# A graph layer on one core: left-over nodes moved to the front, the x part of layer 1 moved ahead of the last slots, iteration 0 written out

## The chip, the cores and the metric

One core of one Trainium2 chip runs the whole kernel. The metric is the device time of one execution in microseconds (us). Before the change it is 276.57 us, the median of three runs (276.30 to 278.17).

## The reference, cut to what matters

```python
agg = jax.ops.segment_sum(edges, recv, num_segments=N_NODES)   # edges [412500, 48] -> [12500, 48]
u = graph_globals[batch]                                       # batch is all zero: one row for every node
h0 = jnp.maximum(_layernorm(x, axis=-1), 0.0)                  # x [12500, 128]
h = jax.nn.relu(jnp.concatenate([h0, agg, u], axis=1) @ W1 + b1)   # 240 -> 256
return x + h @ W2 + b2                                         # 256 -> 128
```

Everything is float32. `recv` (`dst` in the kernel) is sorted, and each node has 33 edges on average (412,500 / 12,500).

## The kernel before, in words

**Chunks, groups, slots.** The edges are cut into chunks of 768 (128 partitions of 6 edges), four chunks make a group, and 1,024 nodes with 11 groups make an iteration. Twelve iterations cover 12,288 nodes and groups 1 to 132; group 0 comes ahead of them and groups 133 and 134 (six chunks) behind them, with the last 212 nodes, called Z or "the rest". In an iteration the 11 groups sit in six slots (`SLOTS`), two groups in each but slot 4. Each slot has its own buffers for edges (`e`), one-hots (`oh`), windows (`pl`) and partial sums (`ss`), and an edge buffer is loaded again, for the next iteration, as soon as the sums that read it are done.

**The segment sum as matmuls.** `onehot` (L662) builds on VectorE, for each edge, a row of 28 that marks its node relative to the chunk's first node. `add_up` (L681) multiplies edges by one-hots on TensorE (L685) and ScalarE copies the sums out of PSUM (L689). `windows` (L669) builds on VectorE where a chunk's 28 sums lie in a window of 186 nodes, and `place` (L695) multiplies the sums by these windows into the aggregate banks `ax` and `ay` (L707), 512 nodes each. A window that crosses the edge of a bank is two matmuls (`pieces`, L44).

**The dst values.** `dst_1`, `dst_2` and `dst_3` (L578 to L611) turn `dst` into the relative positions `rel` and the offsets `off`: for each of five blocks of 128 chunks VectorE casts and subtracts (L583, L586), TensorE transposes (L600), ScalarE copies (L601), and TensorE and VectorE make the offsets (L593, L609). `fetch` and `fetch_off` copy one iteration's part of them.

**The node part.** For each half of an iteration, A and B (512 nodes each): `stats`, `variance` and `shift` on VectorE with a root on ScalarE, `norm` on ScalarE (L735), `turn` transposes on TensorE (L744) with a copy on ScalarE (L745), `layer_x` (L754) and `layer_e` (L759) make layer 1 in banks `ph` and `pt`/`po`, `relu` (L764) on ScalarE, `second` (L780) makes layer 2 into `ph`, VectorE adds x and b2 into `hold` (L784), and all held results are stored at the end. `add_b` (L739) on GpSimd adds b2 to x. `sums_out` (L750) on ScalarE copies the aggregates for `layer_e`.

**What sets the order.** `Flow` collects all operations in one list. Each engine runs its own in the list's order, and `order` works out the semaphore waits from what each operation reads and writes. `run` emits all that stands ahead of iteration 0, then a hardware loop over the iterations for every engine. TensorE has a loop of its own, whose round is cut at `f.mark`: it begins with slot 4 of the iteration before and ends with slot 3. An iteration on TensorE is: sums of slots 0, 1, 2; placing of slot 5's bank 0, slot 0's bank 1 and slot 1; layer 2 of the iteration before, A and B; sums of slot 3, (round ends) 4, 5; the transposes; placing of slots 2, 3, 4, 5; x part; edge part. In iteration 0 layer 2 works on zeros that ScalarE wrote first. The load of the next x is issued by ScalarE after the copies of the transposes; the edge loads by SyncE. In the prologue SyncE issues the five dst blocks, group 0, slots 0 and 1, x, the other slots. The epilogue sums, places and transforms the rest, between the last edge part and the last layer 2, and stores.

Of the kernel before, what the change touches and what calls it, by code (L numbers as in the profile page):

```python
# [13 lines left out]
OP = mybir.AluOpType  # L14
# [18 lines left out]
BACK = 46  # L33
# [21 lines left out]
class Flow:  # L55
# [22 lines left out]
    def order(self, loop):  # L78
# [15 lines left out]
        for o in self.seq:  # L94
# [19 lines left out]
            for n in sorted(deps, reverse=True):  # L114
# [5 lines left out]
                if not inside(o):  # L120
# [31 lines left out]
        self.at_lo = {o["name"]: o["count"] for o in self.seq if o["it"] == lo}  # L152
# [38 lines left out]
    def run(self):  # L191
# [5 lines left out]
        body = [o for o in self.seq if o["it"] == lo]  # L197
        end = [o for o in self.seq if o["it"] is not None and o["it"] > hi]
        for e in self.of:
            self.prepare(e)  # L200
        self.straight([o for o in start if o["eng"] != "PE"])
        regs = {}
        for o in body:
            for n, back in self.body.get(o["name"], []):
                u = self.unit(n)
                key = (o["eng"], u, (self.at_lo[n] - lo - back + self.extra[n]) * u)
                if key not in regs:
                    r = self.of[o["eng"]].alloc_register(f"w_{o['eng']}_{len(regs)}")
                    self.of[o["eng"]].reg_mov(r, key[2] + lo * u)
                    regs[key] = r  # L210

        def ahead(e):
            for n, c in sorted(self.ahead[e].items()):
                self.of[e].wait_ge(self.sem[n], (self.rank[n, c] + self.extra[n]) * self.unit(n))
# [13 lines left out]
        others = [e for e in self.of if e != "PE"]  # L228
        for e in others:
            ahead(e)  # L230
        every = {o["name"] for o in self.seq if o["it"] == hi}
        with nc.Fori(lo, hi + 1, 1, engines=[self.of[e].engine for e in others]) as i:
            for e in others:
                mine = [o for o in body if o["eng"] == e]
                for always, some in groupby(mine, lambda o: o["name"] in every):
# [7 lines left out]
        own = [o for o in body if o["eng"] == "PE"]  # L243
        cut = [o["name"] for o in own].index(self.mark)
        with nc.Fori(0, hi - lo + 2, 1, engines=[nc.tensor.engine]) as j:
# [7 lines left out]
            with nc.tensor.If(j < hi - lo + 1):  # L253
                for o in own[:cut]:
                    repeat(o, None)
# [152 lines left out]
def kernel(  # L408
# [25 lines left out]
    RC = NCH - (NIT * GI + 1) * CG  # L434
    RN = N - NIT * IN
    assert TAIL == TP * T and 0 < RN <= BN and RN % RZ == 0 and RN // RZ <= P
    assert CG < RC <= 2 * CG and IN * (E // N) == IE
# [20 lines left out]
    rel = const.tile([P, ((NIT + 1) * GI + 1) * q], F32)  # L458
    off = const.tile([P, (NIT + 1) * GI + 1], F32)
# [8 lines left out]
    two = (("a", R), ("b", R), ("r", RZ))  # L468
    RR = [r for _, r in two]
    xt = [const.tile([P, r, D], F32, name=f"x{k}") for k, r in two]  # L470
# [5 lines left out]
    ot = [const.tile([P, r, D], F32, name=f"ot{k}") for k, r in two]  # L476
# [5 lines left out]
    hold = [const.tile([P, max(NIT - 1, n) * R * D], F32, name=f"hold{k}") for k, n in (("a", -(-(NB + DF) * CE // (R * D))), ("b", 0))]  # L482
    ssr = const.tile([P, 2, DE], F32)
# [13 lines left out]
    zero = const.tile([P, 1], F32)  # L497
    base = const.tile([P, NIT + 1, GI], F32)
# [8 lines left out]
    fc = [const.tile([P, 1], F32, name=f"fc{k}") for k in range(NB)]  # L507
    mf = [const.tile([P, P // CG], F32, name=f"mf{k}") for k in range(NB)]
# [14 lines left out]
    def load_dst(b):  # L523
# [5 lines left out]
        if full < rows:  # L529
            n = CE // TAIL  # L530
            dma("SP", f"ld{b}r", [], [k + "r"], d[full:rows, :n * TAIL].rearrange("a (n e) -> a n e", e=TAIL),
                dst[None, None, E - TAIL:E].to_broadcast([1, n, TAIL]))
            dma("SP", f"ld{b}s", [], [k + "s"], d[full:rows, n * TAIL:], dst[None, E - TAIL:E - TAIL + CE - n * TAIL])
# [4 lines left out]
    def load_e(s, j, only=None):  # L538

        for k, g in enumerate(SLOTS[s]):  # L540
            if only not in (None, k):
                continue
            dma("SP", f"le{s}.{k}", [], [f"e{s}.{k}"], e[s][:, k * CG:(k + 1) * CG],
# [475 lines left out]
```

## Time and profile before

| what | number |
|---|---|
| median of the runs | 276.57 us |
| the profiled execution: its own time | 279.47 us |
| its span, first to last instruction | 277.7 us |
| TensorE busy, VectorE busy | 256.6 us (92%), 239.2 us (86%) |
| ScalarE busy, GpSimd busy | 127.6 us (46%), 54.5 us (20%) |
| read from HBM, mean rate over the span | 87.75 MB, 339 GB/s |

A row of a group or of the order in time names start, length, engine, source line, operation, output and input tiles with their shapes, and a count; in brackets stand the engine's idle time ahead of it and what ended that. PEld is the weight load of a matmul. A float32 matmul appears as two. "issue" marks time in which the engine waited for nothing that the profile shows.

### The profile page before, as it was taken

The numbers are of one execution on the slowest core, as the hardware profiler recorded it, in microseconds if no ns is written. First come the engines' busy times: TensorE is split into PE (matmuls) and PEld (weight loads), VectorE is DVE, ScalarE is ACT, GpSimd is POOL, SyncE is SP. The second block draws the span as 40 slices with busy tenths as digits, with TensorE's granted clock in tenths as the row PEclk, the third lists the DMA queues.
The fourth block names the chain that finished last, engine by engine and source line by source line (L and its number), as shares of the span: only waits on it lengthen the run. The fifth ranks groups of instructions, "written<-read, shape, count | busy, mean of one in ns | idle before, by whom it ended". The sixth has DMA issues, their size and how long they took to land.

```text
span 277.7 us, 17205 instructions
## 1 busy us (share of the span) xinstructions
PE 256.6 (92%) x7567; PEld 198.7 (72%) x7568; DVE 239.2 (86%) x591; ACT 127.6 (46%) x316; POOL 54.5 (20%) x47
## 2 busy tenths in 40 slices
PE   2787999999999999999999999999999999999991
PEld 2676867858849859768678588497596686785690
DVE  4599999999989989989989899899899799898211
ACT  7710535537347345445363383473454443633510
POOL 8100050140500500501303105005005023043000
PEclk9855899999999999999999999999999999999868
DMA  6999999999999999999999999999999999979402
GB/s 205 319 389 385 371 388 391 390 393 374 389 393 320 390 372 332 390 311 390 392 302 390 393 311 388 392 310 390 361 323 390 327 385 392 308 284 382 173 23 75
DMA packets 79012, 94.33 MB, mean 340 GB/s; under 512 B 3227, under 2 KB 72189, under 8 KB 78998
## 3 DMA queue, kind: packets, MB, share of 16 engines
q1 hardware_dynamic: 75398, 87.63, 90.0%
q10 hardware_dynamic: 3312, 6.03, 5.7%
q0 software_dynamic: 288, 0.49, 0.7%
q8 instruction: 7, 0.11, 0.2%
q14 instruction: 7, 0.06, 0.1%
HBM read 87.75 MB, written 6.40 MB: 339 GB/s over the span
## 4 chain that ended last, share of the span: by engine, by line
PE 88%; DMA 4%; SPq 3%; issue 3%; DVE 0%
PE s L685 28%; PE ph L780 18%; PE ph L754 8%; PE ax L707 7%; PE ph L759 5%; PE po L754 4%; PE pt L754 4%; DMA e<-in_edge_attr_dram 4%; PE pt L759 4%; PE ay L707 3%; SPq L520 3%; PE pt L744 3%; PE po L744 2%; PE s L942 1%; PE s L754 1%
## 5 line engine op out<-in xcount | busy, mean ns | idle before, releaser
L666 DVE TENSOR_TENSOR oh<-iota_v,rel_i 128x1344 f32<-128x1344 f32 (+1 forms) x78 | 130.7, 1715 | 0.0
L685 PEld LDWEIGHTS s<-e,oh 128*28 128x28 f32 x6336 | 75.1, 109 | 20.2 <-issue 18.3
L685 PE MATMUL s<-e,oh 128*28 128x48 f32 x6336 | 80.7, 210 | 8.1 <-issue 6.9
L739 POOL TENSOR_TENSOR xba<-xa,b_sb 128x512 f32<-128x512 f32 x12 | 15.3, 1278 | 196.9 <-DVE holda L784 196.9
L689 ACT COPY ss<-s 128x96 f32<-128x96 f32 (+1 forms) x72 | 16.9, 234 | 67.8 <-PE s L685 67.8
L672 DVE TENSOR_SCALAR pl<-iota_w,off_i 128x186 f32<-128x186 f32 x141 | 35.1, 308 | 0.5
L739 POOL TENSOR_TENSOR xbb<-xb,b_sb 128x512 f32<-128x512 f32 x12 | 31.1, 2590 | 0.0
L780 PEld LDWEIGHTS ph<-w,hida 128*128 128x128 f32 x208 | 26.0, 203 | 4.2 <-issue 4.2
L780 PE MATMUL ph<-w,hida 128*128 128x128 f32 x208 | 28.5, 293 | 0.0
L707 PE MATMUL ax<-pl,ss 128*48 128x186 f32 (+3 forms) x172 | 27.3, 300 | 0.0
L707 PE MATMUL ay<-pl,ss 128*48 128x186 f32 (+3 forms) x168 | 26.4, 298 | 0.0
L764 ACT ACTIVATE hida<-ph,bias 128x512 f32<-128x512 f32 x12 | 8.3, 688 | 39.3 <-PE ph L759 39.3
L780 PE MATMUL ph<-w,hidb 128*128 128x128 f32 x208 | 25.4, 275 | 0.0
L780 PEld LDWEIGHTS ph<-w,hidb 128*128 128x128 f32 x208 | 24.3, 192 | 0.0
L735 ACT ACTIVATE xna<-xa,sha,sca 128x128 f32<-128x128 f32 x48 | 19.8, 483 | 3.1 <-DVE sha L731 2.9
L707 PEld LDWEIGHTS ax<-pl,ss 128*48 128x48 f32 x172 | 17.6, 126 | 4.3 <-issue 2.0
L735 ACT ACTIVATE xnb<-xb,shb,scb 128x128 f32<-128x128 f32 x48 | 19.6, 480 | 0.0
L714 DVE BATCH_NORM_STATS2 sta<-xa 128x6 f32<-128x128 f32 x48 | 10.4, 280 | 9.4 <-DMA xa<-in_x_dram 9.4
L707 PEld LDWEIGHTS ay<-pl,ss 128*48 128x48 f32 x168 | 17.8, 124 | 0.0
L759 PE MATMUL ph<-ags,w1a 48*128 48x512 f32 x48 | 13.6, 641 | 0.0
L754 PE MATMUL ph<-hta,w1h 128*128 128x512 f32 x24 | 13.5, 644 | 0.0
L754 PE MATMUL pt<-hta,w1h 128*128 128x512 f32 x24 | 12.3, 592 | 0.0
(150 smaller groups left out, 305.3 us busy)
## 6 DMA issues: line engine op xcount, KB each, us to landing
e<-in_edge_attr_dram SPq DMA_DIRECT2D x133, 576.0 KB, 8.0
xa<-in_x_dram ACTq DMA_DIRECT2D x11, 256.0 KB, 5.3
xb<-in_x_dram ACTq DMA_DIRECT2D x11, 256.0 KB, 5.8
out_dram<-holda SPq DMA_DIRECT2D x11, 256.0 KB, 3.5
out_dram<-holdb SPq DMA_DIRECT2D x11, 256.0 KB, 3.5
holda<-in_dst_dram SPq DMA_DIRECT2D x4, 384.0 KB, 5.5
e<-in_edge_attr_dram SPq DMA_DIRECT2D x1, 720.0 KB, 4.4
xa<-in_x_dram SPq DMA_DIRECT2D x1, 256.0 KB, 9.5
```

Source lines behind the costliest of these rows:

```text
L666: op("DVE", f"oh{name}", reads + ["iota_v"], [f"oh{name}"], lambda i: [nc.vector.tensor_tensor(ov, iota_v[:, None, None, :].to_broadcast([ ...
L672: nc.vector.tensor_scalar(out[:, j], iota_w, o[j], None, OP.is_equal) for j in range(len(o))])
L685: nc.tensor.matmul(S[k][NV * c:NV * c + V, j * DE:(j + 1) * DE], o[:, (j * CG + c) * T + t], ev[:, j * CG + c, t * DE:(t + 1) * DE], start ...
L689: op("ACT", f"ss{name}", [f"S{k}"], [f"ss{name}"], lambda i: [nc.scalar.copy(sv.rearrange("p j d -> p (j d)"), S[k][:, :m * DE])])
L707: out.append(nc.tensor.matmul(agg[bk][h:h + DE, at:at + w], sv[:, j], pv[:, j, frm:frm + w], start=bk in fresh and bk not in seen, stop=Tr ...
L714: op("DVE", f"st{k}", [f"x{k}", f"x{k}t"], [f"st{k}"], lambda i: [nc.vector.bn_stats(st[k][:m, r], xt[k][:m, r]) for r in range(RR[k])])
L735: nc.scalar.activation(xn[k][:m, r], xt[k][:m, r], AF.Relu, bias=sh[k][:m, r:r + 1], scale=sc[k][:m, r:r + 1]) for r in range(RR[k])])
L739: nc.gpsimd.tensor_tensor(xb[k][:m], xt[k][:m], b2_sb[:m, None, :].to_broadcast([m, RR[k], D]), OP.add)])
L744: op("PE", f"tu{k}", [f"xn{k}", "ident"], [key], lambda i: [nc.tensor.transpose(pv[:, r, :m], xn[k][:m, r], ident[:m, :m]) for r in range( ...
L754: nc.tensor.matmul(o, w1h[:, a * P:(a + 1) * P], hT[k][:, :, :m], start=first, stop=False, skip_group_check=True)])
L759: nc.tensor.matmul(o, w1a[h:h + DE, a * P:(a + 1) * P], ag[k // 2][h:h + DE, :, :m], start=False, stop=True, skip_group_check=True)])
L780: nc.tensor.matmul(ov[:m, r], hid[k][:, a, r, :m], w2[:, a], start=(a == 0), stop=(a == NH - 1)) for r in range(RR[k]) for a in range(NH)])
```

## The change

The 212 left-over nodes become the first 212. Their three groups (0 to 2; `HG`) are loaded right behind the first dst block, into buffers of slots 4 and 5, and summed, placed and put through both layers in the new `head`, which interleaves this work with the dst blocks; the loads of dst blocks 1 to 4 stand behind these groups. For blocks 1 to 4 the subtraction moves from VectorE to ScalarE. The windows start 72 nodes ahead instead of 46. Iteration 0 (`first`) is emitted ahead of the loops on all engines but TensorE, with its statistics among the prologue's one-hots, and on TensorE layer 2 is skipped in that iteration. SyncE's program is written out for all iterations. In every iteration the transposes stand behind slot 3, the x part behind slot 4, and slot 5, the placing and the edge part behind that; TensorE's round is cut at slot 5; ScalarE issues the next x load behind slot 5's copy. The last edge load waits for the 84-edge tail. The epilogue keeps layer 2 of A and B, the stores and the check of the ranges.

```diff
-BACK = 46
+HG = 3
+BACK = 72
...
+            with nc.tensor.If(j < hi - lo + 1):
+                for always, some in groupby(own[:cut], lambda o: o["name"] in at_first):
+                    with ExitStack() as later:
+                        if not always:
+                            later.enter_context(nc.tensor.If(j > 0))
+                        for o in some:
+                            repeat(o, None)
...
+HEAD = ((5, 0), (5, 1), (4, 0))
+def load_head():
+    for g, (s, k) in enumerate(HEAD):
+        dma("SP", f"leh{g}", [], [f"e{s}.{k}"], e[s][:, k * CG:(k + 1) * CG], rows_e(g * GE, GE))
...
+            op("DVE", f"nf{b}", [f"fc{b}"], [f"nf{b}"], lambda i: [nc.vector.tensor_scalar(nf[b][:rows], fc[b][:rows], -1.0, -(V - 1) / 2, OP.mult, OP.add)])
+            op("ACT", f"df{b}", src + [f"nf{b}"], [f"df{k}"], lambda i: [nc.scalar.activation(df[k][:rows], d[:rows], AF.Identity, bias=nf[b][:rows])])
...
+    def head():
+        load_dst(0)
+        load_head()
+        load_x(Z, lambda i: 0, m_z, eng="SP")
+        for b in range(1, NB):
+            load_dst(b)
+        load_e(0, 1)
+        load_e(1, 1)
+        load_x(A, lambda i: RN, eng="SP")
+        load_x(B, lambda i: RN + BN, eng="SP")
+        load_e(2, 1)
+        load_e(3, 1)
...
+        dst_1(0)
+        dst_td(0)
+        dst_of(0)
...
+            op("PE", f"suh{g}", [f"ohh{g}", f"e{s}.{k}"], ["S1"], ...
...
+        load_e(4, 1)
+        load_e(5, 1)
...
+        dst_1(1)
+        dst_td(1)
+        dst_of(1)
+        op("PE", "bi", ["w1u", "u"], ["PH1"], ...
+        op("PE", "pcz", ["ssr"] + [f"plh{g}" for g in range(HG)], ["bk1"], ...
+        op("ACT", "agz", ["bk1"], ["ag2"], ...
+        stats(Z, m_z)
+        variance(Z, m_z)
+        dst_1(2)
+        dst_td(2)
+        dst_of(2)
+        fetch(1)
+        onehots(0)
+        shift(Z, m_z)
+        norm(Z, m_z)
+        dst_1(3)
+        dst_td(3)
+        dst_of(3)
+        onehots(1)
+        op("PE", "tu2", ["xn2", "ident"], ["Z0"], ...
+        op("ACT", "hT2", ["Z0"], ["hT2"], ...
+        dst_1(4)
+        dst_td(4)
+        dst_of(4)
+        fetch_off(1)
+        op("DVE", "bj", ["PH1", "b1"], ["bias"], ...
+        places(0)
+        places(1)
+        for a in range(NH):
+            layer_x(f"z{a}", zk[a], zr[a], Z, a, True, m_z)
+        for a in range(NH):
+            layer_e(f"z{a}", zk[a], zr[a], Z, a, m_z)
+        for a in range(NH):
+            relu(f"z{a}", zk[a], zr[a], Z, a, m_z)
+        add_b(Z, m_z)
+        onehots(2)
+        f.at = 0
+        for k in (A, B):
+            stats(k)
+            variance(k)
+        f.at = -1
+        onehots(3)
...
+        onehots(4)
+        onehots(5)
+        second(Z, m_z, S[1][:, HG * DE:], "Z1")
+        places(2)
...
+    def first():
+        farthest()
+        fetch(1)
+        add_slots(0, 1, 2)
+        onehots(0)
+        onehots(1)
+        onehots(2)
+        norm(A)
+        norm(B)
+        place(5, (0,), 0)
+        place(0, (1,))
+        place(1)
+        places(5)
...
+        rest()
+
+    def rest():
+        add_slots(3)
+        turn(A)
+        turn(B, P, po, "PO")
+        add_slots(4)
+        layers(layer_x)
+        add_slots(5)
+        for s in (3, 4, 5):
+            onehots(s)
+        next_x()
+        for s in (2, 3, 4):
+            place(s)
+        place(5, (), 1)
+        sums_out(A)
+        sums_out(B)
+        for s in (2, 3, 4):
+            places(s)
+        layers(layer_e)
+        layers(relu)
...
-    f.mark = "su4"
+    f.mark = "su5"
```

More of the change, by code (lines that the diff above doesn't have):

```diff
@@ L855, in prologue @@
+        op("ACT", "agz", ["bk1"], ["ag2"], lambda i: [
+            nc.scalar.copy(ag[1][:DE, :, :m_z], agg[1][:DE, :RN].rearrange("p (c r) -> p r c", r=RZ))])
+        stats(Z, m_z)
[3 more added lines that the diff above has]
+        dst_of(2)
         fetch(1)
         onehots(0)
-        onehots(1)
-        windows(5, pl[5], ["off0"], [off[:, 0:1], off[:, 0:1]])
-        op("PE", "bi", ["w1u", "u"], ["PH1"], lambda i: [
-            nc.tensor.matmul(ph[1][:, NG + a:NG + a + 1], w1u[:, a * P:(a + 1) * P], u, start=True, stop=True, skip_group_check=True) for a in range(NH)])
@@ new lines, in head, with add_slots @@
+        op("DVE", "spare", [], ["spare"] + [f"di{b}" for b in range(NB)] + [f"di{NB - 1}r", f"di{NB - 1}s"] + [f"df{k}" for k in range(DF)]
+           + [f"{n}{g}" for n in ("ohh", "plh") for g in range(HG)],
+           lambda i: [nc.vector.memset(hold[0][:, 0:1], 0.0)])
+        op("DVE", "f0", rz, ["farm"], lambda i: [nc.vector.tensor_reduce(farm, rel[:, :HG * q], AX.X, OP.max, apply_absolute_value=True)])
+    def add_slots(*some):
+        for s in some:
+            sums(s)
+            if f.at < NIT - 1:
+                load_e(s, 1)
@@ L973 @@
     flag_of = {r.engine: r for r in flags}
-    prologue()
-    for it in range(NIT):
+    head()
+    first()
+    for it in range(1, NIT):
         body(it)
```

285 lines of the change are left out of this document (139 added, 146 removed).

## The prediction

> **What bounds the kernel now.** I read the page first, then its span cut into stages, then TensorE, ScalarE and VectorE through one steady iteration, then the head and the tail the same way. An iteration is one round of eleven slot groups; it begins with the 96 sums of slot 0 (L685).
>
> ```profile
> GB/s 205 319 389 385 371 388 391 390 393 374 389 393 320 390 372 332 390 311 390 392 302 390 393 311 388 392 310 390 361 323 390 327 385 392 308 284 382 173 23 75
> ```
> ```profile
> 0.00:16.68 16.68, 9.72 (x92) 8.69 (x94) 10.35 (x34) 11.36 (x20) 7.25 (x22) 0.87 0.88 283
> 16.68:43.76 27.08, 23.69 (x612) 18.55 (x613) 26.61 (x66) 8.02 (x22) 3.83 (x2) 0.77 1.08 384
> 257.29:277.70 20.41, 14.24 (x133) 11.34 (x131) 3.83 (x15) 4.28 (x11) 0.00 (x0) 0.77 0.24 85
> ```
> ```profile
> 43.76:257.29 213.53, 208.95 (x6734) 160.09 (x6733) 198.39 (x479) 103.91 (x265) 43.39 (x23) 1.00 1.03 363
> ```
>
> Each stage row gives its length, then the busy time of TensorE, its weight loads, VectorE, ScalarE and GpSimd, then the granted clock, the DMA share and GB/s; the GB/s row above cuts the span into 40 slices of 6.94 us. Four stages: 16.68 us before the first sums, 27.08 us for iteration 0, 213.53 us for iterations 1 to 11 (19.41 us each), 20.41 us of tail. In the long stage TensorE lacks only 4.58 us of being busy throughout, so TensorE's order is the time there; VectorE has 15 us to spare, the DMA engines little. One iteration on TensorE, ScalarE and VectorE:
>
> ```profile
> 82.67 3.49 PE L685 MATMUL s<-e,oh 128*28 128x48 f32 x288
> 87.18 2.05 PE L780 MATMUL ph<-w,hida 128*128 128x128 f32 x16
> 90.94 1.22 PE L685 MATMUL s<-e,oh 128*28 128x48 f32 x96
> 92.57 1.73 PE L685 MATMUL s<-e,oh 128*28 128x48 f32 x144 [0.40 <-issue]
> 94.24 0.66 PE L744 MATMUL pt<-ident,xna 128*128 128x128 f32 x4
> 95.26 0.36 PE L707 MATMUL ax<-pl,ss 128*48 128x186 f32 x1
> 96.51 1.13 PE L754 MATMUL ph<-hta,w1h 128*128 128x512 f32 x2
> 100.14 1.13 PE L759 MATMUL ph<-ags,w1a 48*128 48x512 f32 x4
> 102.06 1.14 PE L685 MATMUL s<-e,oh 128*28 128x48 f32 x88
> ```
> ```profile
> 94.36 0.24 ACT L689 COPY ss<-s 128x96 f32<-128x96 f32 x1 [0.82 <-PE s L685]
> 95.64 0.34 ACTq L520 DMA_DIRECT2D xa<-in_x_dram  x1
> 96.17 0.34 ACTq L520 DMA_DIRECT2D xb<-in_x_dram  x1
> 96.55 0.58 ACT L750 COPY ags<-ax 48x512 f32<-48x512 f32 x1 [0.55 <-PE ay L707]
> 97.15 0.58 ACT L750 COPY ags<-ay 48x512 f32<-48x512 f32 x1
> ```
>
> Two things to see. The 0.40 us before slot 4 is the branch at the end of TensorE's loop round: short sums stand on both sides of it, so its sequencer has nothing queued ahead. And the two copies of the aggregates (L750, done at 97.73) cost nothing, because the x part (L754, 96.51 to 100.14) runs between the placing (L707) and the edge part (L759) that reads them.
>
> **The change part by part: steady iterations.** TensorE's new order is slot 3, transposes, slot 4, x part, [branch], slot 5, placing, edge part. Let S be the end of slot 5. First, the branch now stands behind 3.63 us of queued x part, so its 0.42 us (4.58 / 11) is hidden: -0.42. Second, nothing is left between placing and edge part. On ScalarE the x loads stay ahead of the copies: slot 5's copy starts at S+0.1, the two DMA issues follow (95.64 to 96.51 now, 0.9), the first aggregate copy starts at about S+1.3 and ends at S+1.9, the second at S+2.5. The placing takes 1.25 us (95.26 to 96.51), so TensorE waits from S+1.25 to S+2.0, then again briefly for the second copy, and ends its edge part at S+3.95 instead of S+3.18: +0.77. Third, with BACK 72 four of the eleven windows cross a bank edge instead of three: one matmul more, about 0.05. Net +0.40 us; over eleven iterations **+4.4 us**.
>
> The x load is moved too: it now stands on ScalarE's queue behind slot 5's copy, that is behind the x part. VectorE needs it:
>
> ```profile
> 100.94 0.87 DVE L714 BATCH_NORM_STATS2 sta<-xa 128x6 f32<-128x128 f32 x4 [0.99 <-DMA xa<-in_x_dram]
> ```
> ```profile
> 26.02 0.86 DVE L714 BATCH_NORM_STATS2 sta<-xa 128x6 f32<-128x128 f32 x4
> 35.60 0.68 DVE L784 TENSOR_TENSOR holda<-ph,xba 128x512 f32 x1
> ```
> ```profile
> out_dram<-ota SPq DMA_DIRECT2D x1, 256.0 KB, 2.0
> xa<-in_x_dram ACTq DMA_DIRECT2D x11, 256.0 KB, 5.3
> ```
>
> From the statistics to the end of the hold addition, which frees the x part's bank, VectorE takes 10.3 us. So there is a ring: S, issue at +0.4, landing, 10.3, x part 3.63, slot 5 1.15: 15.5 us plus the landing. TensorE's own round is 19.8 us, so the ring stays hidden while x lands within 4.3 us. The rows bracket that: 2.0 us for a store with the engines idle, 5.3 us with five edge loads queued ahead. An iteration of 19.8 us asks 7.01 MB, 18.0 us at 390 GB/s, so after the start the queue runs empty before S, and I take a landing nearer the idle row, 3.4 us; the ring costs nothing. The Trainium skill ("DMA: Bandwidth & Descriptors", section "Anatomy of one DMA") gives a fixed 2 us plus the bytes at 436 GB/s, an estimate of 2.6 us here: by it the sum stays, while by 5.3 us every iteration would take 20.8. The trace disagrees with the page for a load behind others.
>
> **The head.** SyncE now queues dst block 0, three groups (1.77 MB), the left-over x (0.11 MB), then dst 1 to 4. Block 1 thus has 2.66 MB ahead and with it, and 0.49 MB of weights come meanwhile. By the GB/s row, 1.42 MB pass by 6.94 us and 319 GB/s follow: 12.4 us. The row below says how far completion lags: 5.09 MB including weights had to pass for a load that landed at 19.61, against 17.6 by the GB/s row. (That sum: dst 1.65, five groups of 0.59, weights 0.49.) I take 14.4 us, where block 1 is used at 5.10 now. The edge slots land 1.3 MB, 3.4 us, later as well, the last at about 36, before their sums as timed below.
>
> ```profile
> 9.50 10.11 DMA e<-in_edge_attr_dram
> ```
> ```profile
> 2.45 1.12 ACT L830 COPY hida<-zero 128x512 f32<-128x512 f32 x2
> 6.54 0.85 ACT L601 COPY rel<-pt 128x384 f32<-128x384 f32 x1 [0.90 <-PE pt L600]
> 7.18 0.91 ACT L601 COPY rel<-ph 128x384 f32<-128x384 f32 x1
> 30.81 1.65 ACT L735 ACTIVATE xna<-xa,sha,sca 128x128 f32<-128x128 f32 x4 [1.33 <-DVE sha L731]
> ```
> ```profile
> 5.10 0.15 DVE L583 CAST fc<-holda 128x1 f32<-128x1 int32 x1
> ```
> ```profile
> 5.62 0.88 PE L600 MATMUL pt<-ident,holda 128*128 128x128 f32 x3
> 10.64 0.62 PE L600 MATMUL ph<-ident,holda 128*128 128x128 f32 x3
> 15.54 1.01 PE L860 MATMUL ph<-u,w1u 64*128 64x1 f32 x4
> ```
> ```profile
> 261.95 1.78 PE L754 MATMUL s<-htr,w1h 128*128 128x212 f32 x4
> 265.37 3.40 PE L780 MATMUL ph<-w,hida 128*128 128x128 f32 x16
> ```
>
> From there one chain winds through ScalarE, which now does the dst subtraction (0.87, an estimate from the 512-wide copies), and TensorE, whose program puts all left-over work before slot 0. Block 1: cast and constant 0.4, subtraction 0.9, transposes, offsets, bias and three placings 3.9, copy and root of the left-overs 0.65: 20.3. Block 2: subtraction 0.9, transposes 0.9, two copies 1.55, norm 0.9: 24.4. Block 3: 0.9, 0.9, 1.55, copy of the transposed x 0.3: 28.1. Block 4: 0.9, transposes 1.0, offsets 0.5: 30.4. Then left-over layer 1 twice 1.7, relu 0.8, layer 2 1.7 (half of 3.4): slot 0 starts at **36.3 us** instead of 16.68. These are half-clock durations, and I keep them because the stretches below show the clock at 0.50 through bursts like these. VectorE waits too: the bias (bj) reads the bank that block 4's offsets write last, so placings and one-hots of slots 0 to 2 stand behind it until 30.4; that still leaves slot 2's one-hot at about 33, in time.
>
> ```profile
> 12.22:24.24 12.02, 8.92 (x258) 7.83 (x258) 11.88 (x24) 3.08 (x8) 0.00 (x0) 0.50 1.08 385
> 24.24:29.28 5.04, 5.04 (x112) 4.30 (x113) 4.79 (x26) 0.63 (x4) 0.00 (x0) 0.50 1.09 371
> ```
>
> The Trainium skill ("TensorE: Matmul & The Clock Gate", Part 1) says that the clock is released after about 3.4 us of sustained work. The trace asked for 5.04 us of unbroken work; by the page's figure slot 0 would start 1.7 us earlier.
>
> Iteration 0 then runs without the two layer-2 blocks on zeros (3.8 us of TensorE at full clock; 4.2 in iteration 0 now) and mostly without DMA waits: slots 0 to 2 3.45, copy 0.25, the norms, queued behind that copy, 3.2, transposes 0.5, slot 4 0.6, x part 3.6, slot 5 1.15, then 3.95 as above: 16.7 us. Iteration 1 starts at 53.1 instead of 43.76: **+9.3 us**. Both ends: with the full-clock rows (0.62 for three transposes) 31.5 for slot 0, and with block 1 landing 3 us earlier as well 28.5, so +1.5; with half clock lasting through slots 0 to 2, +13.
>
> **The tail.** Left-over sums, placing and layers are gone.
>
> ```profile
> 257.69 0.69 ACT L764 ACTIVATE hida<-pt,bias 128x512 f32<-128x512 f32 x1
> 271.42 0.37 ACTq L520 DMA_DIRECT2D out_dram<-otb  x1
> ```
> ```profile
> 270.69 0.69 DVE L782 TENSOR_TENSOR otb<-ph,xbb 128x512 f32<-128x512 f32 x1 [0.84 <-PE ph L780]
> ```
>
> After the edge part ends at T (now 257.29), relu is ready at T+1.1, the two layer-2 blocks take 3.8, addition 0.7, issue and landing 2.2, and 3.8 us from the last landing (273.9) to the end of the span: T+11.7, against 20.4. The held stores (22 of 256 KB, 15 us at 385 GB/s) start about 16 us before T and are covered. **-8.7 us.** SyncE's program is written out, which is worth nothing, since no wait above ends on its issuing. Before its very last edge load it now waits for the 16 KB tail to land, some 2 us; behind it stand that load, needed an iteration later, and the held stores, covered as said. The memset and iota moves on GpSimd stand in its first 8 us, ahead of anything that block 1 lets through, and cost nothing either.
>
> **The sum.** +9.3 + 4.4 - 8.7 = +5.0: a span of 282.7 instead of 277.7. The profiled execution took 279.47, 2.9 above the median of the three runs; against the median 276.57 + 5.0 = **281.6 us**.
>
> **Rivals.** (1) The head is short: full clock and block 1 early, slot 0 at 28.5. Then +1.5 + 4.4 - 8.7 gives 273.8, faster. For it: left-over work fills an idle TensorE (9.72 busy of 16.68). Against it: the chain is serial over three engines whatever the clock. It decides below a start of about 31. (2) The aggregate copies are covered after all: 0.77 less per iteration, 273.1, faster. For it: two 0.58 us copies are small beside 1.25 us of placing, if they could begin with its first bank. Against it: on ScalarE's queue two DMA issues stand ahead of them, and no TensorE work stands between placing and edge part. (3) x keeps landing after 5.3 us: the ring makes 20.8, eleven times 1.0 more, 292.6. For it: the row's median over all iterations; it decides from 4.3 us on.
>
> **How the numbers follow.** Forecast 0.50 (own range 277 to 287: slower 0.40, within 0.10), rival 1 0.17 (faster 0.08, within 0.09), rival 2 0.12 (faster 0.09, within 0.03), rival 3 0.18 (slower), rivals 1 and 2 together 0.03 (265, faster). Faster 0.20, within 0.22, slower 0.58, with 1%, 2.8 us, as what a measurement of this kernel can tell. The range 271 to 290 leaves out half of rival 3, the joint case and the lower parts of rivals 1 and 2, together under 0.2.
>
> **What would show it.** In the new profile: the first L685 sums of slot 0 start near 36; TensorE waits about 0.6 us before the edge part with the aggregate copy as releaser; no 0.4 us issue gap remains; the idle time before the statistics is short after the second iteration; the span ends 11.7 us after the last edge part. I am wrong if slot 0 starts before 31, if the edge part follows the placing without a wait, or if iterations 1 to 11 take over 20.3 us each.

## The result and the profile after

The changed kernel takes 309.63 us (median of 4 runs, 307.69 to 311.63) against 276.64 us: 1.118 times the time, 95% interval 1.110 to 1.127. The forecast was 281.6 with a range to 290; slower was right, the size was not. The profiled execution took 311.63 us with a span of 309.8. A few executions, among them the profiled one of `old_order` below (297.96 us), fell in a slower state and are left out of the times and ratios.

The span of the changed kernel by stages: its head (up to the first sums of slot 0), iteration 0, iterations 1 to 11, the tail; then two stretches of iteration 0. Columns as before: length, busy time of TensorE, its weight loads, VectorE, ScalarE, GpSimd, then granted clock, DMA share, GB/s.

```profile
0.00:44.26 44.26, 20.52 (x212) 17.41 (x214) 26.25 (x88) 14.21 (x29) 10.39 (x27) 1.00 0.74 250
44.26:69.85 25.59, 20.37 (x583) 14.71 (x583) 12.82 (x24) 8.06 (x21) 0.00 (x0) 0.87 0.76 242
69.85:295.78 225.93, 215.96 (x6755) 162.77 (x6754) 199.71 (x476) 106.22 (x265) 41.85 (x22) 1.00 0.98 339
295.78:309.80 14.02, 3.95 (x34) 3.73 (x33) 1.71 (x4) 1.02 (x2) 0.00 (x0) 0.82 0.12 43
```
```profile
44.26:54.02 9.76, 4.92 (x263) 4.59 (x264) 3.74 (x5) 0.48 (x2) 0.00 (x0) 0.91 0.68 221
54.02:59.13 5.11, 5.11 (x136) 3.97 (x135) 3.18 (x8) 3.32 (x9) 0.00 (x0) 0.51 0.71 234
```

| stage | before | forecast | after | after less forecast |
|---|---|---|---|---|
| iteration 1 starts at | 43.76 | 53.1 | 69.85 | +16.8 |
| iterations 1 to 11 | 213.53 (19.41 each) | 217.9 (19.81) | 225.93 (20.54) | +8.0 |
| tail | 20.41 | 11.7 | 14.02 | +2.3 |

The last column adds up to the 27.1 us between the forecast span of 282.7 and 309.8. TensorE was all but busy throughout in the long stage; it now idles for 10 of 225.93 us there, and for more than half of the head.

**The head.** VectorE's and TensorE's rows around the start of slot 0 in the changed kernel; in square brackets the idle time before an instruction and what ended it.

```profile
32.38 0.16 DVE L945 TENSOR_TENSOR bias<-ph,b_sb 128x2 f32<-128x2 f32 x1 [6.08 <-PE ph L631]
43.47 0.26 DVE L654 TENSOR_TENSOR vv<-ph,base 128x103 f32<-128x103 f32 x1
```
```profile
36.29 2.04 PE L824 MATMUL s<-w,hidr 128*106 128x128 f32 x8 [0.53 <-ACT hidr L808]
44.26 2.97 PE L729 MATMUL s<-e,oh 128*28 128x48 f32 x135 [5.93 <-DVE vv L654]
47.90 1.95 PE L729 MATMUL s<-e,oh 128*28 128x48 f32 x127 [0.67 <-issue]
54.02 0.80 PE L729 MATMUL s<-e,oh 128*28 128x48 f32 x26 [4.16 <-issue]
```

The left-over work ends on TensorE at 38.3, but slot 0 waits 5.93 us more for the conversion of the offsets of blocks 1 to 4 (vv), which now stands near the end of VectorE's head. Before its loop, TensorE waits once for everything in the head that any instruction of its loop depends on (`ahead("PE")`), and one of these, the x part, writes the bank that vv reads. Inside slots 1 and 2 TensorE then stands for 0.67 and 4.16 us with no wait that the profile shows ("issue").

**A steady iteration** of the changed kernel, from the end of slot 5's sums to the next: timeline rows of ScalarE, TensorE, VectorE and SyncE, each in a fence, and last the page's DMA issues (count, KB each, median us from issue to landing).

```profile
127.47 0.24 ACT L733 COPY ss<-s 128x96 f32<-128x96 f32 x1 [4.69 <-PE s L729]
127.75 0.42 ACTq L545 DMA_DIRECT2D xa<-in_x_dram  x1
128.35 0.34 ACTq L545 DMA_DIRECT2D xb<-in_x_dram  x1
128.73 0.58 ACT L794 COPY ags<-ax 48x512 f32<-48x512 f32 x1 [1.02 <-PE ay L751]
```
```profile
127.34 0.36 PE L751 MATMUL ax<-pl,ss 128*48 128x186 f32 x1
129.36 1.30 PE L803 MATMUL ph<-ags,w1a 48*128 48x512 f32 x3 [0.67 <-ACT ags L794]
131.88 3.27 PE L729 MATMUL s<-e,oh 128*28 128x48 f32 x288
143.42 1.10 PE L798 MATMUL ph<-hta,w1h 128*128 128x512 f32 x2 [0.54 <-DVE holda L828]
147.02 1.18 PE L729 MATMUL s<-e,oh 128*28 128x48 f32 x92
```
```profile
132.66 0.87 DVE L758 BATCH_NORM_STATS2 sta<-xa 128x6 f32<-128x128 f32 x4 [1.68 <-DMA xa<-in_x_dram]
142.59 0.69 DVE L828 TENSOR_TENSOR holda<-ph,xba 128x512 f32 x1
```
```profile
127.47 0.92 SPq L578 DMA_DIRECT2D e<-in_edge_attr_dram  x2
```
```profile
xa<-in_x_dram ACTq DMA_DIRECT2D x11, 256.0 KB, 4.7
xb<-in_x_dram ACTq DMA_DIRECT2D x11, 256.0 KB, 5.8
```

The ring that the prediction named is closed in this iteration: x issued at 127.75, statistics at 132.66, hold addition to 143.28, x part from 143.42, slot 5 from 147.02. As to why x is late, the SyncE row shows that the end of slot 5, which lets ScalarE issue x, also lets SyncE issue two edge loads of 576 KB, within the same microsecond. Nor had the earlier loads drained: from 127.50 to 128.00 the DMA engines still move 392 GB/s, at a share of 1.08. Which of the two delays x was not tried apart.

The ring is not the only limit. From the start of the placing (127.34) to the end of the edge part (131.88) TensorE takes 4.54 us, where the forecast had 3.95. Two group rows of the changed kernel, and between them the one of the kernel before, show what it loses (count, busy time, mean ns of one, then idle time before and what ended it):

```profile
L803 PE MATMUL ph<-ags,w1a 48*128 48x512 f32 x48 | 20.7, 641 | 7.4 <-ACT ags L794 7.4
L759 PE MATMUL ph<-ags,w1a 48*128 48x512 f32 x48 | 13.6, 641 | 0.0
L798 PE MATMUL ph<-hta,w1h 128*128 128x512 f32 x24 | 13.2, 633 | 3.0 <-DVE holda L828 2.9
```

TensorE waits 7.4 us for the aggregate copies, and the first group of the edge part is drawn out from 13.6 to 20.7 us; the hold addition that ends the ring costs it 2.9 us. In three of the ten iterations TensorE does not wait for the hold addition, and these take 20.26 to 20.36 us; the other seven take 20.58 to 20.87. So TensorE's own round, with the exposed copies, is about 20.26 us, and the ring adds 0.33 on the mean.

The page's chain that ended last, in shares by engine, shows how much of the changed kernel now hangs on VectorE and on DMA:

```profile
PE 44%; DVE 24%; DMA 17%; ACT 4%; issue 4%; ACTq 2%; SPq 1%; DVEq 0%
```

### The profile page after: what moved, and what is told of

It reads as the page before. It is cut to its first block, busy times and chain, and to the rows that moved or that the text cites. A ratio compares the mean times of both kernels' runs of the same rounds, so it can differ in the third digit from the quotient of the medians.

```text
span 309.8 us, 16941 instructions
## 1 busy us (share of the span) xinstructions
PE 260.8 (84%) x7581; PEld 198.6 (64%) x7582; DVE 240.5 (78%) x591; ACT 129.5 (42%) x315; POOL 52.2 (17%) x49
## 4 chain that ended last, share of the span: by engine, by line
PE 44%; DVE 24%; DMA 17%; ACT 4%; issue 4%; ACTq 2%; SPq 1%; DVEq 0%
PE s L729 14%; DVE oh L710 12%; DMA xb<-in_x_dram 12%; PE ph L798 8%; PE ph L824 6%; DMA holda<-in_dst_dram 4%; DVE pl L716 4%; PE po L798 3%; PE pt L798 3%; ACTq L545 2%; PE ph L803 2%; DVE stb L758 2%; PE ax L751 2%; DMA xa<-in_x_dram 2%; DVE holda L828 1%
## 5 line engine op out<-in xcount | busy, mean ns | idle before, releaser
L710 DVE TENSOR_TENSOR oh<-iota_v,rel_i 128x1344 f32<-128x1344 f32 (+1 forms) x78 | 130.3, 1694 | 16.3 <-PE s L729 16.1
L729 PEld LDWEIGHTS s<-e,oh 128*28 128x28 f32 x6336 | 73.6, 109 | 32.9 <-issue 31.6
L783 POOL TENSOR_TENSOR xbb<-xb,b_sb 128x512 f32<-128x512 f32 x12 | 29.6, 2471 | 0.0
L751 PE MATMUL ay<-pl,ss 128*48 128x186 f32 (+4 forms) x168 | 28.0, 300 | 0.0
L751 PE MATMUL ax<-pl,ss 128*48 128x186 f32 (+1 forms) x192 | 27.9, 288 | 0.0
L803 PE MATMUL ph<-ags,w1a 48*128 48x512 f32 x48 | 20.7, 641 | 7.4 <-ACT ags L794 7.4
L779 ACT ACTIVATE xna<-xa,sha,sca 128x128 f32<-128x128 f32 x48 | 19.8, 483 | 14.7 <-DVE sha L775 14.7
L824 PEld LDWEIGHTS ph<-w,hida 128*128 128x128 f32 x192 | 22.3, 191 | 4.4 <-issue 3.1
L824 PE MATMUL ph<-w,hida 128*128 128x128 f32 x192 | 24.6, 281 | 0.5 <-ACT hida L808 0.5
L824 PE MATMUL ph<-w,hidb 128*128 128x128 f32 x192 | 23.4, 275 | 0.0
L758 DVE BATCH_NORM_STATS2 sta<-xa 128x6 f32<-128x128 f32 x48 | 10.5, 280 | 16.1 <-DMA xa<-in_x_dram 16.1
L824 PEld LDWEIGHTS ph<-w,hidb 128*128 128x128 f32 x192 | 22.4, 192 | 0.0
L803 PEld LDWEIGHTS ph<-ags,w1a 48*128 48x128 f32 x48 | 7.1, 184 | 13.0 <-ACT ags L794 13.0
```

Of the source, the lines that this page charges most:

```text
L710: op("DVE", f"oh{name}", reads + ["iota_v"], [f"oh{name}"], lambda i: [nc.vector.tensor_tensor(ov, iota_v[:, None, None, :].to_broadcast([ ...
L729: nc.tensor.matmul(S[k][NV * c:NV * c + V, j * DE:(j + 1) * DE], o[:, (j * CG + c) * T + t], ev[:, j * CG + c, t * DE:(t + 1) * DE], start ...
L751: out.append(nc.tensor.matmul(agg[bk][h:h + DE, at:at + w], sv[:, j], pv[:, j, frm:frm + w], start=bk in fresh and bk not in seen, stop=Tr ...
L758: op("DVE", f"st{k}", [f"x{k}", f"x{k}t"], [f"st{k}"], lambda i: [nc.vector.bn_stats(st[k][:m, r], xt[k][:m, r]) for r in range(RR[k])])
L779: nc.scalar.activation(xn[k][:m, r], xt[k][:m, r], AF.Relu, bias=sh[k][:m, r:r + 1], scale=sc[k][:m, r:r + 1]) for r in range(RR[k])])
L783: nc.gpsimd.tensor_tensor(xb[k][:m], xt[k][:m], b2_sb[:m, None, :].to_broadcast([m, RR[k], D]), OP.add)])
```

## The experiments

Each kernel was compared with runs of the kernel before on the same chip (276.5 to 277.4 us). "Iteration" is the mean of ten starts of slot 0, 20.59 us in the changed kernel (69.85 to 275.76). One caution: with an unchanged head, slot 0 started between 41.5 and 45.7 us in six profiles, so stage lengths and waits are compared rather than starts. The code cuts are shortened.

**1. The order of an iteration: undone, and done alone.**

```diff
 def rest():
-    add_slots(3); turn(A); turn(B, ...); add_slots(4); layers(layer_x); add_slots(5)
-    onehots 3, 4, 5; next_x()
+    add_slots(3, 4, 5); onehots 3, 4, 5; turn(A); turn(B, ...); next_x()
     place ...; sums_out(A); sums_out(B); places ...
+    layers(layer_x)
     layers(layer_e); layers(relu)
```

> The changed kernel with slots 3, 4, 5, the transposes, the placing, the x part and the edge part in the old order in every iteration, x issued behind the transposes' copies as before; head and tail stay changed, and TensorE still waits for the offset conversion before slot 0. Theory 1, the new order is the whole loss in the steady stage (20.59 us an iteration in the changed kernel's trace, 69.85 to 275.76 in ten, against 19.41 before): an iteration of about 19.45, 11 x 1.15 = 12.6 us less, 297 us. Rival, something else in the change costs it (SyncE's loads written out, windows that cross a bank edge more often, the loop that begins at 1): still 20.5 an iteration, 309 us. My own term of +0.40 an iteration, if the rest came from elsewhere: 305 us.

Here the cut of TensorE's round is behind slot 3 again, and one added dependency keeps its wait for the offset conversion. Measured: 293.39 us, the median of three (1.061 times before, 1.055 to 1.066), an iteration of 19.26.

> The kernel before with the new order of one iteration alone: slot 3, transposes, slot 4, x part, loop branch, slot 5, x issue, placing, aggregate copies, edge part. Theory 1: +1.15 us an iteration here too, in twelve iterations 13 to 14 us, about 290 us. My term on record, +0.40 an iteration: 281 us. Rival, the order costs only beside the new head: within 1% of 276.6.

Measured: 291.94 us (1.053, 1.048 to 1.058), iteration 20.50; iteration 0 grew from 27.08 to 31.23, with issue gaps of 2.32 and 3.27 us between its first slots. So the new order alone costs 1.1 to 1.3 us an iteration on either kernel, about three times my +0.40. In the kernel before, too, TensorE then waits 7.4 us for the copies, and only 1.0 us for the hold addition.

**2. x against the aggregate copies.** In the changed kernel, x issued earlier; and the copies ahead of x.

```diff
-        layers(layer_x); add_slots(5); ...; next_x(); ...
+        layers(layer_x); next_x(); add_slots(5); ...            # x_early
```
```diff
-        next_x(); place ...; sums_out(A); sums_out(B)
+        place ...; sums_out(A); sums_out(B); next_x()           # ag_first
```

> The changed kernel with the two x loads issued on ScalarE between the copies of slot 4 and slot 5 instead of behind slot 5's. Ring theory (x lands 4.3 to 6.2 us after an issue at S+0.4 and S+1.0, and the statistics, one-hots and hold addition of the next iteration hang on it): the wait of VectorE for x falls from 1.5 us an iteration to under 0.4, and the two issues no longer stand ahead of the aggregate copies: 19.6 to 19.9 us an iteration, 300 to 303 us. Rival, the x loads now wait on ScalarE's queue for GpSimd's two additions (2.6 us each, behind the hold addition) and hold slot 5's copy back: no gain, 308 us or more. Rival, x is not on the path: VectorE's wait moves, the iteration stays over 20.3, 307 us.

Measured: 304.05 us (1.098, 1.093 to 1.102), iteration 19.95, all ten within 0.01. VectorE's wait for x is gone, as the row of its group says (count, busy time, mean ns of one, then idle time before and what ended it):

```profile
L758 DVE BATCH_NORM_STATS2 sta<-xa 128x6 f32<-128x128 f32 x48 | 10.4, 278 | 0.0
```

> The changed kernel with the two aggregate copies ahead of the two x issues on ScalarE's queue. Ring theory: x is issued 1.5 to 2 us later, and the whole ring with it, so the edge part's wait for the copies shrinks, but the iteration grows by 0.9 to 1.9 us: 320 us or more. Copies theory (the exposed 0.62 us between placing and edge part is the loss, x is not on the path): 0.6 us an iteration less, about 303 us.

Measured: 320.83 us (1.156, 1.151 to 1.161), iteration 21.47. TensorE's wait for the copies fell from 7.4 to 4.3 us in all, VectorE's for x rose from 16.1 to 28.2 (the groups of this kernel):

```profile
L803 PE MATMUL ph<-ags,w1a 48*128 48x512 f32 x48 | 20.7, 641 | 4.3 <-ACT ags L794 4.3
L758 DVE BATCH_NORM_STATS2 sta<-xa 128x6 f32<-128x128 f32 x48 | 10.5, 281 | 28.2 <-DMA xa<-in_x_dram 28.2
```

In `ag_first` the two waits move in opposite directions and the time follows x: TensorE's wait for the hold addition is 11.6 us there, so the ring binds once x is late enough. `x_early` is no test of the ring alone, because its x issues no longer stand ahead of the copies on ScalarE: TensorE's wait for the hold addition is gone (2.9 us before), and its wait for the copies also fell, from 7.4 to 4.3 us. In the steady rows the copies' wait fell from 0.67 to 0.36 us, so of the 0.64 us gained about half is the ring and half the copies.

**3. The copies covered.** x early, and half of the x part behind the placing:

```diff
-        layers(layer_x); next_x(); add_slots(5)
+        layers(layer_x, (0, 1)); next_x(); add_slots(5)
...
+        layers(layer_x, (2, 3))
         layers(layer_e)
```

> The changed kernel with x issued between the copies of slots 4 and 5 (as in the earlier kernel that took 19.95 us an iteration) and the second half of the x part (1.71 us of TensorE) moved to between the placing and the edge part. Theory, the 0.69 us that were left against the old order are the exposed aggregate copies (0.36 us of wait and an edge part of 2.5 us instead of 1.9) less the hidden loop branch (0.40): both costs go, the branch stays hidden: 18.9 to 19.2 us an iteration, 293 to 296 us. Rival, the rest is something else in the new order (the slots' banks, the copies' place in the queue): 19.8 or more, 303 us.

Measured: 294.69 us (1.065, 1.058 to 1.071), iteration 19.12, so 0.83 us come from covering the copies. The iteration is now 0.14 shorter than in the old order (19.26), but the whole times, 294.69 and 293.39, are the same within their spread. The edge part's first group in this kernel, with no wait left and back at its length of before:

```profile
L803 PE MATMUL ph<-ags,w1a 48*128 48x512 f32 x48 | 13.5, 641 | 0.0
```

> The kernel before with the new order of its iterations, x early and the x part split, the same way; nothing else of the change. Theory: 19.0 to 19.2 us an iteration instead of 19.41, so 2.5 to 4.5 us less in iterations 1 to 11; iteration 0 grew by 4.1 us with the new order alone, and if it does so again, 276 to 279 us; if it keeps 27 us, 272 to 274.

Measured: 275.90 us (0.996, 0.992 to 0.999), iteration 19.25, iteration 0 28.73. This is the one version that is not slower than the kernel before: its median is 0.4% below, less than the spread of one kernel's runs. In its eleven steady iterations (46.00 to 257.76) TensorE never idles, as the row of that stretch shows (columns as above):

```profile
46.00:257.76 211.76, 211.76 (x6734) 159.58 (x6733) 194.61 (x470) 103.49 (x265) 43.38 (x23) 1.00 1.03 362
```

**4. The head: VectorE's order.** The offset conversion right behind its fetch and the left-over's addition ahead of slot 3's one-hots; then (`vv_bj`) the bias addition ahead of the left-over placing too, with the conversion behind slot 2's one-hots. In both, an added dependency makes TensorE wait for the left-over's addition.

```diff
         fetch_off(1)
+        dst_3(ph[1], "PH1", range(1, NB))                       # vv_early
         ... bj ...
+        second(Z, ...)
         onehots(3)
...
-        second(Z, ...)
         places(2); places(3); places(4)
-        dst_3(ph[1], "PH1", range(1, NB))
```

> The changed kernel with the conversion of the offsets of blocks 1 to 4 moved on VectorE to right behind their fetch (ahead of the bias addition), and the left-over nodes' last addition ahead of slot 3's one-hots; TensorE must wait for both before slot 0, and for nothing later on VectorE. Theory: TensorE's wait of 5.93 us before slot 0 falls to 0.7 or less (the left-over layer 2 ends at 38.33, its addition 0.5 later), and if iteration 0 keeps its 25.6 us the time falls by 5.2 to 304.4. Rival: iteration 0 is held by something else that doesn't move (edge loads, one-hots, the norms), and stretches: 307.5 or more.

Measured: 303.13 us (1.096, 1.090 to 1.102). TensorE's wait is 1.00 us instead of 5.93, and iteration 0 kept its length (25.16). Slot 0's row of the first of the two kernels:

```profile
38.49 2.94 PE L729 MATMUL s<-e,oh 128*28 128x48 f32 x134 [1.00 <-DVE otr L826]
```

> As the kernel with the earlier conversion, and the bias addition moved ahead of the left-over placing as well, with the conversion behind slot 2's one-hots, so that VectorE doesn't wait for block 4's offsets before the placings and one-hots of slots 0 to 2 (6.08 us of idle time there). Theory: VectorE's idle time moves or goes, but slot 0 still waits for TensorE's own chain to 38.3, so the same time as that kernel within 1 us. Rival: the VectorE wait was on the path, 3 us or more less than that kernel.

Measured: 302.87 us (1.093, 1.088 to 1.099), slot 0 at 38.18: the same within 0.3 us. The 6.08 us that VectorE waits at the bias addition cost only through what stood behind it.

**5. The head: order of the loads and of TensorE.**

```diff
-        load_dst(0); load_head(); load_x(Z, ...); load_dst(1) ... load_dst(4)
+        load_dst(0) ... load_dst(4); load_head(); load_x(Z, ...)    # dst_first
```

> The changed kernel with all five dst blocks first in SyncE's queue, ahead of the three head groups and the left-over x. Theory, the head is a serial chain that starts when block 1 lands (16.35): block 1 lands before 8, the head groups 3.4 us later (leh2 at 17.5), so the placing of the left-overs at about 20 as now, but blocks 2 to 4 wait for nothing: slot 0 starts 2 to 5 us earlier, 305 to 307 us. Rival, the chain is bound by the head groups and by the engines, not by dst: within 1 us of 309.6.

Measured: 311.31 us (1.125, 1.119 to 1.132): no gain, as the rival has it, and 1.7 us above the changed kernel where the rival allowed 1. Block 1 landed at 5.9 instead of 16.35, but its transposes started at 19.78, later than in the changed kernel (17.74). They waited for ScalarE's subtraction (18.78 to 19.73), which in ScalarE's program stands behind the copies of the head sums (18.52 to 18.89); the head sums, whose groups now land last, stand ahead of the transposes in TensorE's program as well (TensorE's rows, the last head sum and block 1's first transposes):

```profile
17.28 1.18 PE L898 MATMUL s<-e,holdb 128*28 128x48 f32 x48 [0.67 <-DMA e<-in_edge_attr_dram]
19.78 0.93 PE L643 MATMUL po<-ident,holda 128*128 128x128 f32 x3 [1.32 <-ACT holda L624]
```

So I gave the engines' programs the same order as the loads: `head_re`, with all dst blocks, then the head sums, and the two moves of experiment 4; `best` adds the old order of the iterations; `best2` also moves the dst subtraction back to VectorE (`if b == 0` becomes all blocks), the left-over transposes behind the head sums, and the head's one-hots between the blocks; `best3` is that head with the split order of experiment 3. `best_f`, `best2` and `best3` hold back the first edge loads (experiment 6).

```text
         dst blocks 0 to 4: dst_1, dst_td, dst_of
         bj; dst_3(ph[1], ...); left-over statistics, norm, transposes
         head sums; left-over placing, layers 1; onehots 0 to 3; second(Z, ...)
```

> The changed kernel with its head in another order: SyncE loads the five dst blocks, then the left-over x, then the three head groups; TensorE does all five blocks' transposes and offsets first, then the first left-over layer-1 product, the head sums as they land, the placing and the rest of the left-over work; the offset conversion, the bias addition and the left-over's last addition stand ahead of what TensorE's wait must not include. Steady iterations stay in the new order. Theory, the head's 44.26 us are the order of its work, not its amount: the last head group lands at 17.1 (as with dst first), its sums, placing, layers and addition take about 8.5 us, slot 0 starts at 26 to 28; if iteration 0 keeps its 25.6 us, 291 to 294 us. Rival, the amount of work on VectorE and ScalarE or the edge loads then hold slot 0 or iteration 0 instead: 298 us or more.

Measured: 301.17 us (1.085, 1.079 to 1.090), slot 0 at 35.65: the rival. A dst block took 3.24 us (transposes at 11.72, 14.96, 18.20 in the next kernel), going round ScalarE and TensorE.

> That head, with the old order of the iterations. If the two add up, the 15.3 us that the old order gave on the changed kernel come off: 276 to 279 us, level with the kernel before. Rival, with the old order iteration 0 is bound by the norms and late edge loads, and part of the head's gain is lost there: 283 us or more.

Measured: 288.91 us (1.042, 1.036 to 1.047): the rival again. The iteration is 19.38, 1.12 less than in `head_re`, but iteration 0 has the gap of experiment 6.

> The kernel with the reordered head, the old order and the delayed first edge loads (285.6 us, slot 0 at 35.5), with the dst subtraction of all blocks on VectorE, as before the change, and the left-over transposes behind the head sums on TensorE. Theory, that head ran at 3.24 us a block because ScalarE does the subtraction (0.94) and two copies (0.85 each) in turn with TensorE, and the left-over norm stood behind it: blocks at 2.5 us or less, slot 0 at 27 to 30, 278 to 281 us. Rival, VectorE, which has the one-hots too, becomes the bound of the head: slot 0 at 33 or later, 283 us or more.

Measured: 281.81 us (1.018, 1.012 to 1.023), slot 0 at 30.67, 4.8 earlier than in `best_f`: between theory and rival.

> That head with the new order, x early and the split x part instead of the old order. If the iteration takes 19.0 us instead of 19.38 as in the reordered kernels with the old order, 4 us less than that kernel: 274 to 277 us, at or below the kernel before (277). If the split gives nothing over the old order, 278 to 281.

Measured: 282.00 us (1.018, 1.013 to 1.023): a miss. Its iteration is 19.12, as expected, but iteration 0 took 24.12 us against 20.23, with a gap of 3.38 us in slot 1 again.

**6. The gap in iteration 0.** SyncE waits for slot 2's sums before the first edge load of iteration 0.

```diff
+                if it == 1 and (s, k) == (0, 0):
+                    nc.sync.wait_ge(f.sem["su2"], f.value(dict(name="su2", count=1)))
                 made.append(nc.sync.dma_start(e[s]..., rows_e(...)))
```

> The changed kernel with SyncE waiting for slot 2's sums of iteration 0 before it issues the first edge loads of that iteration, so that no edge load is in flight while TensorE works through slots 0 to 2. Theory, the 4.16 us gap in slot 2's sums (ended by nothing but issue) is an instruction fetch that stands behind the edge loads just issued: the gap falls to 1.5 us or less and the time by about 2.5 to 3, to 307. Rival, the gap is a fixed cost of first passing through that code: 3.5 us or more stays, and the time stays at 309 or rises with the later loads.

Measured: 307.30 us (1.109, 1.100 to 1.118); the gap in slot 2 is 0.87 us instead of 4.16, with 1.98 in slot 3, and iteration 0 is 23.43 instead of 25.59. All issue gaps of slots 1 to 3 together are 4.05 us against 4.83, so only part of the gain is in the gaps; from 50.75 on the granted clock is 1.00, where in the changed kernel it is 0.51 until 59.13. TensorE's rows in slots 2 and 3 of this kernel:

```profile
50.75 0.54 PE L731 MATMUL s<-e,oh 128*28 128x48 f32 x26 [0.87 <-issue]
55.13 0.65 PE L731 MATMUL s<-e,oh 128*28 128x48 f32 x41 [1.98 <-issue]
```

> As the last one, with SyncE waiting for slot 2's sums before the first edge loads of iteration 0. If the instruction fetch is again the gap in slots 1 and 2, 2.3 us less than that kernel, 274 to 277 us; if the edge loads are late by then (less time between the head and iteration 1), no gain or up to 3 us more.

Measured: 285.57 us (1.027, 1.023 to 1.032), 3.3 less than `best`; the gap, in these two kernels ahead of slot 3, is 1.34 us instead of 3.44. Twice the gap shrinks when the edge loads are held back. In `fetch_clear` the DMA engines move nothing during the short gap (49.90 to 50.75) and 311 GB/s during the longer one (53.10 to 55.13). In the trace of the changed kernel a packet of 16 KB of the instruction queue runs from 51.67 to 52.62, within the gap from 49.85 to 54.02. In all fourteen traces with the new head, such a packet ends 1.2 to 1.7 us before TensorE's first sums after the longest gap of slots 1 to 3. That this packet holds TensorE's next instructions and waits behind the edge loads is argued from these times; nothing names its content. In `best3` the edge loads that the head itself issues land up to the gap, which would explain it there, but that was not tried apart.

## Why the prediction was wrong, step by step

- **Loop branch hidden, -0.42: right.** No issue gap is left in the steady iterations.
- **Aggregate copies exposed, +0.77: right in kind, too small; the first step that failed in the steady stage.** The edge part ends 4.54 us after the start of the placing (127.34 to 131.88), not 3.95. TensorE's first wait is 0.67 us, near the 0.75 of the forecast; but for the second copy the forecast had "again briefly" and next to nothing, and the edge part takes 2.52 us (129.36 to 131.88) instead of the 1.92 of before. Together 1.27 us instead of 0.77. TensorE's own round came to 20.26 us instead of 19.81, and this, not the ring, is most of what the steady stage lost: 0.85 us an iteration over the kernel before. Experiment 3 shows it: with the copies covered the iteration is 19.12.
- **x landing in 3.4 us, the ring hidden: the second step that failed there.** x lands in 4.7 and 5.8 us (medians), and in no kernel here in under 4.3. The premise that the queue runs empty before S did not hold: the DMA engines move 392 GB/s until 128.00, past S. I also did not ask what slot 5's end itself releases, which is two edge loads in the same microsecond. The row that I set aside (5.3 us) was the better bound. The ring added 0.33 us an iteration in the profiled execution; in the profiles of the five variants that keep the changed kernel's order of the iterations, the iteration took 20.3 to 20.5, so it varies.
- **Rival 3: the right mechanism, its size in part luck.** Its 20.8 us an iteration lie close to the 20.59 measured, but it took TensorE's own round as 19.8. The exposed copies had already made that 20.26, which this rival did not contain.
- **Slot 0 at 36.3: the step that failed in the head.** Two parts. Block 1 landed at 16.35 instead of 14.4, and the chain behind it, of the forecast length, ended 2.0 us late, at 38.33. The other 5.93 us are a wait that I did not list: I followed what TensorE does before slot 0, not what it waits for there. I had looked at the bias addition's wait and judged it by the one-hots behind it; the conversion behind it was the one that counted. Experiment 4 removed 4.93 us of it. And "a chain from block 1's landing" was only half the cause: experiment 5 shows that an early block 1 alone gains nothing, since the programs of ScalarE and TensorE hold the copies of the head sums and the sums themselves in front of it.
- **Iteration 0 in 16.7 us: failed by 8.9.** Slots 0 to 2 were to take 3.45 us; with the gaps of 0.67 and 4.16 us, which the forecast put at nothing, the third slot's sums end only at 54.8. TensorE works from 54.02 to 59.13 at a clock of 0.51. I bounded the half clock, but saw no gap, though the kernel before has one of 1.76 us in the same slots.
- **Zero blocks skipped, left-overs out of the tail: right in kind.** Neither could pay for what the head lost: even `best2`, with the head reordered, starts iteration 1 at 50.9 us, the kernel before at 43.76.
- **Tail 11.7: 2.3 too short.** The last store was issued at 300.99 and landed 2.0 us later, 7.3 us after the edge part's end, close to the forecast of 7.9. From there to the end of the span it took 6.8 us instead of the 3.8 that I carried over from before. The trace has SyncE, whose program is now written out, take a last branch at 303.53 us and start its next instruction only at 307.15; in the kernel before, that step is 274.55 to 275.07. Packets of the instruction queue run in between (304.41 to 305.68). From the last landing to the end it is 6.8 to 7.4 us in all fourteen kernels with the changed program and 3.7 in the three with the program of before. Which part of the program costs it was not tried; the forecast had put SyncE's written-out program at nothing.
- **Rivals 1 and 2 were wrong** for the reasons given against them. The condition "over 20.3 us an iteration" was met.

## What to carry to other kernels

When a copy between two matmul groups loses its cover, price the whole group that reads it, not only its first wait: here the rest of the group lost 0.60 us, nearly as much as that wait. When a load is moved, take its landing from rows of the same loop, not from a transfer alone, and list what else the same event releases. When work is moved into a head, look for the one wait that gathers the whole head before a loop, and for the last instruction on every other engine that it includes; an order of loads helps only where each engine's program has the same order. When a copy stands between two matmul groups, split an independent group over both sides of it, rather than moving it whole.

## What the runs showed of the hardware

- A short load among others: 256 KB took 2.0 to 2.4 us nearly alone (the two stores of the tail), and 4.3 to 5.8 (medians) as x load inside the loop, in every kernel here. The estimate of 2.6 us from the Trainium skill ("DMA: Bandwidth & Descriptors", section "Anatomy of one DMA") is for a transfer by itself, and its fit is for transfers that GpSimd issues; the medians inside the loop stay far from it.
- In the gap of iteration 0 the clock fell back, and it stayed at 0.51 through 5.11 us in which TensorE was busy throughout, as long as the 5.04 us before the change. In the traces the half clock lasts 6.83 us here (52.21 to 59.03), and 3.41, 6.83 or 17.07 us in the other kernels that show it inside the run: one, two or five times 3.41. The Trainium skill ("TensorE: Matmul & The Clock Gate", Part 1) has about 3.4 us of sustained work, counted in a window that runs free of the kernel; the traces agree with the window, and the busy time until the release is longer than 3.4 us in both stretches.
- In the kernel before, TensorE loses 0.11 us at each of the two boundaries between slots 0, 1 and 2 in every steady iteration (288 sums in 3.49 us); with the changed program these sums take 3.27. The 0.22 us would cover the step from 19.41 to the 19.26 of the changed kernel with the old order; in `best`, with the same 3.27, the iteration is 19.38, since the 144 sums of slots 4 and 5 take 1.84 there instead of 1.73. What makes either difference was not tried.
